# A spiking-recommender kernel: five gather tiles for three, the identity built first, small reciprocals, 15 table chunks held

## The chip, the core and the metric

The kernel runs on one core of a Trainium2 chip. The core has five engines that run side by side and meet at semaphores: TensorE (PE in the profile; its weight loads are PEld), VectorE (DVE), ScalarE (ACT), GpSimd (POOL) and SyncE (SP). SP and POOL issue DMAs, which run on the core's 16 DMA engines. The metric is device time in microseconds (us) of one execution, median of several runs.

## What is computed

The reference takes sequences of item numbers (1024 x 50), their lengths, and a table of 100,001 embeddings of 128 numbers. Cut to what matters:

```python
emb = emb_table.at[0].set(0.0)
prefix = jnp.cumsum(emb[seq], axis=1)                 # over the 50 steps
uF = prefix / jnp.minimum(t_idx, lengths)[:, :, None]
y = (uF - mean) * rsqrt(var + eps) * gamma + beta     # mean and var over the 1024 sequences
v = v + (x - v) / 2; spike = (v >= 1); v = v - spike  # one step of the scan over t, x = y[:, t]
uF_out = spikes.mean(axis=0)
scores = uF_out @ emb.T                               # 1024 x 100001
```

## The kernel before

**Two stages.** The first runs over the 50 steps and ends with `countR`, the number of spikes of every dimension (128 partitions) and sequence (1024 columns). The second multiplies `countR` with the whole table and writes the 409.6 MB of scores. The order of instructions on each engine is the program's own (`manual_schedule`); every engine takes its queue in order. Buffers come from pools that hand tiles out in rotation: a tile's writer waits until the last reader of that buffer's earlier tile is done.

**Setup.** SP loads the item numbers `idx` (L106), the lengths spread to all partitions, `len_i` of 128 x 1024 (L108), row 0 of the table, gamma and beta, and then issues `fetch` for the first `AHEAD` = 16 chunks of the table (2048 rows, 1 MB each). POOL issues `gather(0)` and then builds the identity `ident` that TensorE transposes with. VectorE builds `isz` (which places hold item 0), TensorE transposes it (L143), VectorE copies it to `zT` (L145). `rlen`, the reciprocal of the lengths, is worked out on 128 x 1024 by a conversion (L157) and a reciprocal (L158).

**One step t of the first stage.** POOL gathers step t+1 (L209 calls `gather`, L122): eight indirect DMAs, each of 128 table rows, into a tile `e` of 128 x 1024, from a pool of three tiles. `isz` is a tile of that pool too. TensorE transposes the tile's eight blocks into two PSUM banks `pre`, where the running sum over the steps stands (L219). VectorE scales each half to `uF` (L228) and takes its statistics (L229). TensorE subtracts row 0's part for the next step (`correct`, L179, two matmuls) and adds the spikes of the step before to `count` (L189, two matmuls). VectorE and ScalarE then do the normalisation and the neuron's update (L233 to L267) on 128 x 1024. So a step has twelve matmuls, each with its own weight load. In the steps t = 40, 42, 44 and 46 `prepare` (L90 to L92) follows: eight transposes of table rows on TensorE, a copy `hi` on ScalarE and a rest `lo` on VectorE. They stand in the queues ahead of the transposes of steps 41, 43, 45 and 47.

**The second stage** takes 49 chunks of 2048 table rows. For each of eight blocks of 128 sequences, TensorE multiplies (L301), VectorE and ScalarE take turns at moving results to `o` (L309, L311), and SP writes 1 MB to `scores` (L313). After the fifth block of a chunk SP issues `fetch` for the chunk that lies `AHEAD` further on, into the tile of a chunk that has been used.

Of the kernel before, what the change touches and what calls it, by code (L numbers as in the profile page):

```python
# [12 lines left out]
F32 = mybir.dt.float32  # L13
BF16 = mybir.dt.bfloat16
F32R = mybir.dt.float32r
I32 = mybir.dt.int32
# [4 lines left out]
P = 128  # L21
BN_EPS = 1e-5
V_TH = 1.0
CH = 2048
AHEAD = 16
HALF = 1024
BANK = 512

# [2 lines left out]
def rec_kernel(  # L31
# [9 lines left out]
    nc = tc.nc  # L41
    B, T = seq.shape
    N, D = table.shape
    NB = B // P
# [6 lines left out]
    embp = ctx.enter_context(tc.tile_pool(name="embT", bufs=4))  # L51
    rowp = ctx.enter_context(tc.tile_pool(name="rows", bufs=AHEAD))


    countR = const.tile([P, B], F32R, tag="countR", name="countR")
    ident = const.tile([P, P], F32, tag="ident", name="ident")
# [5 lines left out]
    def fetch(c0):  # L62
        w = min(CH, N - c0)
        full, rest = divmod(w, P)
        r = rowp.tile([P, CH // P, D], F32, tag="rows", name=f"rows_{c0}")
        if full:
            nc.sync.dma_start(
                out=r[:, :full, :],
                in_=table[c0 : c0 + full * P, :].rearrange("(k p) d -> p k d", p=P),
            )  # L70
        if rest:
            nc.sync.dma_start(out=r[:rest, full, :], in_=table[c0 + full * P : c0 + w, :])
        rows[c0] = r

    def prepare(c0, h0, pt):


        w = min(CH, N - c0)
        hw = min(HALF, w - h0)
        r = rows[c0]  # L80
        if c0 == 0 and h0 == 0:
            nc.vector.memset(r[0:1, 0, :], 0.0)
        hi = embp.tile([P, HALF], F32R, tag="hi", name=f"hi_{c0}_{h0}")
        lo = embp.tile([P, HALF], F32R, tag="lo", name=f"lo_{c0}_{h0}")
        if hw % 2:
            nc.vector.memset(hi[:, hw : hw + 1].bitcast(F32), 0.0)
            nc.vector.memset(lo[:, hw : hw + 1].bitcast(F32), 0.0)
        for k0 in range(0, hw, P):
            kw = min(P, hw - k0)
            nc.tensor.transpose(pt[:, k0 : k0 + kw], r[:kw, (h0 + k0) // P, :], ident[:kw, :kw])  # L90
        nc.scalar.copy(hi[:, :hw], pt[:, :hw])  # L91
        nc.vector.tensor_tensor(lo[:, :hw], pt[:, :hw], hi[:, :hw].bitcast(F32), ALU.subtract)  # L92
        split[c0, h0] = hi, lo


    with ExitStack() as ph:
        once = ph.enter_context(tc.tile_pool(name="once", bufs=1))
        gp = ph.enter_context(tc.tile_pool(name="gather", bufs=3))
        up = ph.enter_context(tc.tile_pool(name="uF", bufs=2))
        sp = ph.enter_context(tc.tile_pool(name="stats", bufs=3))  # L100
        lp = ph.enter_context(tc.tile_pool(name="lif", bufs=2))
# [1 line left out]
        vp = ph.enter_context(tc.tile_pool(name="v", bufs=1, space=bass.MemoryType.PSUM))  # L103

        idx = once.tile([P, NB, T], I32, tag="idx", name="idx")
        nc.sync.dma_start(out=idx, in_=seq.rearrange("(n p) t -> p n t", p=P))  # L106
        len_i = up.tile([P, B], I32, tag="uF", name="len_i")
        nc.sync.dma_start(out=len_i, in_=lengths.rearrange("(o b) -> o b", o=1).to_broadcast([P, B]))  # L108
        r0 = once.tile([P, D], F32, tag="r0", name="r0")
        nc.sync.dma_start(out=r0, in_=table[0:1, :].to_broadcast([P, D]))  # L110
        gb = once.tile([P, 2], F32, tag="gb", name="gb")
# [1 line left out]
        nc.sync.dma_start(out=gb[:, 1:2], in_=beta.rearrange("(d o) -> d o", o=1))  # L113
        for c0 in range(0, min(AHEAD * CH, N), CH):
            fetch(c0)
# [3 lines left out]
        def gather(t):  # L119
            es[t] = gp.tile([P, B], F32, tag="e", name=f"e_{t}")  # L120
            for n in range(NB):
                nc.gpsimd.indirect_dma_start(  # L122
                    out=es[t][:, n * P : (n + 1) * P],
                    out_offset=None,
                    in_=table,
                    in_offset=bass.IndirectOffsetOnAxis(ap=idx[:, n, t : t + 1].bitcast(U32), axis=0),
                )

        gather(0)
        make_identity(nc, ident)  # L130
        ident_h = once.tile([P, P], BF16, tag="ident_h", name="ident_h")
        nc.vector.tensor_copy(ident_h, ident)

# [7 lines left out]
        zps = vp.tile([P, B], F32, tag="v1", name="zps")  # L141
        for n in range(NB):
            nc.tensor.transpose(zps[:, n * P : (n + 1) * P], isz[:, n, :], ident)  # L143
        zT = once.tile([P, B], F32R, tag="zT", name="zT")
        nc.vector.tensor_copy(zT, zps)  # L145
        r0hi = once.tile([P, D], F32R, tag="r0hi", name="r0hi")
        nc.scalar.copy(r0hi, r0)
        r0n = once.tile([P, D], F32, tag="r0n", name="r0n")
# [4 lines left out]
        nc.vector.tensor_tensor(sel, ident[:, : P // 2], ident[:, P // 2 :], ALU.add)  # L153


        rlen = once.tile([P, B], F32, tag="rlen", name="rlen")
        nc.vector.tensor_copy(rlen, len_i)  # L157
        nc.vector.reciprocal(rlen, rlen)  # L158

        hgb = once.tile([P, 2], F32, tag="hgb", name="hgb")  # L160
        nc.vector.tensor_scalar_mul(hgb, gb, 0.5)
# [45 lines left out]
        for t in range(T):  # L207
# [3 lines left out]
            e = es.pop(t)  # L211
# [3 lines left out]
            uF = up.tile([P, B], F32, tag="uF", name=f"uF_{t}")  # L215
# [74 lines left out]
    for c0 in range(0, N, CH):  # L290
        w = min(CH, N - c0)
        for n in range(NB):
            o = op.tile([P, CH], F32, tag="o", name=f"o_{c0}_{n}")
# [21 lines left out]
            if n in (1, 4) and c0:  # L315
                h0 = 0 if n == 1 else HALF
                if nxt + h0 < N:
                    prepare(nxt, h0, psum.tile([P, HALF], F32, tag="ps", name=f"pt_{nxt}_{h0}"))
            if n == 4 and c0 + AHEAD * CH < N:
                fetch(c0 + AHEAD * CH)  # L320

# [18 lines left out]
```

## Time and profile before

| what | value |
|---|---|
| median of 3 runs (lowest, highest) | 1724.94 us (1724.48, 1726.58) |
| the profiled execution | 1723.19 us, span 1721.3 us |
| first stage: until the writing of scores sets in | 598.5 us, the first 68 us of it beside the loading of 16 chunks |
| second stage | 1122.8 us |
| busy: PE, DVE, ACT, POOL | 1141.8, 969.4, 636.3, 379.5 us |
| POOL's gathers | 400 x 947 ns |
| moved by DMA | 488.75 MB, of it 409.60 MB written to HBM |

The profile is of one execution. A group of instructions is named by its line, engine, operation and tiles (out<-in). After its busy time stand the engine's idle time before it and what ended that; "remote" means that no instruction in the profile fits the semaphore that ended the wait, "issue" that the engine waited for nothing that the profile shows. [...] The step t is also called tile t, after its tile of gathered rows.

### The profile page before, as it was taken

The numbers are of one execution on the slowest core, as the hardware profiler recorded it, in microseconds if no ns is written. First come the engines' busy times: TensorE is split into PE (matmuls) and PEld (weight loads), VectorE is DVE, ScalarE is ACT, GpSimd is POOL, SyncE is SP. The second block draws the span as 40 slices with busy tenths as digits, with TensorE's granted clock in tenths as the row PEclk, the third lists the DMA queues.
The fourth block names the chain that finished last, engine by engine and source line by source line (L and its number), as shares of the span: only waits on it lengthen the run. The fifth ranks groups of instructions, "written<-read, shape, count | busy, mean of one in ns | idle before, by whom it ended". The sixth has DMA issues, their size and how long they took to land.

```text
span 1721.3 us, 13874 instructions
## 1 busy us (share of the span) xinstructions
PE 1141.8 (66%) x4526; PEld 820.3 (48%) x4526; DVE 969.4 (56%) x1261; ACT 636.3 (37%) x698; POOL 379.5 (22%) x406
## 2 busy tenths in 40 slices
PE   2233333433344478877788777877778888888886
PEld 1112222221222356655566555666556666666664
DVE  5557756765667645554455444554445555555554
ACT  1222222221223344443444434444334444444443
POOL 7666666666666000000000000000000000000000
PEclk9855555555555599999999999998998899999999
DMA  9811111111111199999999999999999999999998
GB/s 267 234 44 48 48 48 44 48 49 46 45 49 46 38 391 397 401 400 393 388 394 402 394 391 393 395 400 390 396 396 390 403 410 414 402 405 406 403 402 349
DMA packets 98004, 488.75 MB, mean 284 GB/s; under 512 B 14827, under 2 KB 16652, under 8 KB 48780
## 3 DMA queue, kind: packets, MB, share of 16 engines
q1 hardware_dynamic: 85132, 461.63, 68.9%
q0 software_dynamic: 12800, 26.24, 5.3%
q8 instruction: 35, 0.57, 0.1%
q14 instruction: 37, 0.30, 0.0%
HBM read 78.21 MB, written 409.60 MB: 283 GB/s over the span
## 4 chain that ended last, share of the span: by engine, by line
DMA 48%; DVE 23%; PE 10%; another core or an unknown queue 9%; ACT 5%; issue 4%; POOL 0%; ACTq 0%; DVEq 0%; SPq 0%
DMA scores<-o 48%; PE po L301 9%; DVE bs L229 4%; ACT o L311 4%; DVE uF L228 4%; DVE v L267 3%; DVE s L199 3%; DVE negv L266 2%; DVE o L309 2%; ACT v L264 1%; DVE mv L233 1%; DVE a L257 1%; DVE r L255 1%; DVE q L254 0%
## 5 line engine op out<-in xcount | busy, mean ns | idle before, releaser
L301 PE MATMUL po<-hi,countR 128*128 128x512 f32 x1568 | 679.9, 434 | 179.5 <-ACT o L311 176.4
L309 DVE TENSOR_SCALAR o<-po 128x1024 f32<-128x1024 f32 x392 | 478.9, 1222 | 460.3 <-DMA scores<-o 428.3
L301 PE MATMUL po<-lo,countR 128*128 128x512 f32 x1568 | 645.0, 412 | 0.0
L311 ACT ACTIVATE o<-po 128x1024 f32<-128x1024 f32 (+1 forms) x392 | 399.9, 1020 | 633.2 <-DMA scores<-o 506.0
L301 PEld LDWEIGHTS po<-hi,countR 128*128 128x128 f32 x1568 | 316.0, 202 | 330.5 <-ACT o L311 243.0
L122 POOL DMA_INDIRECT e<-in_L_rec_emb_table,idx x400 | 378.8, 947 | 184.7 <-issue 109.3
L301 PEld LDWEIGHTS po<-lo,countR 128*128 128x128 f32 x1568 | 316.4, 202 | 60.1
L179 PE MATMUL pre<-zT,l 128*128 128x512 f32 x100 | 72.7, 729 | 264.4 <-DVE uF L228 196.0
L179 PEld LDWEIGHTS pre<-zT,l 128*128 128x128 f32 x100 | 27.0, 271 | 306.0 <-issue 192.2
L92 DVE TENSOR_TENSOR lo<-pt,hi 128x1024 fp32r<-128x1024 f32 x98 | 119.7, 1221 | 87.9 <-ACT hi L91 86.2
L228 DVE SCALAR_TENSOR_TENSOR uF<-rlen,pre 128x512 f32<-128x512 f32 x100 | 67.9, 679 | 144.8 <-remote 129.3
L237 ACT ACTIVATE r<-mv,eps 128x1 f32<-128x1 f32 x50 | 14.7, 295 | 351.4 <-DVE mv L233 307.2
L90 PE MATMUL pt<-ident,rows 128*128 128x128 f32 x782 | 108.4, 283 | 19.3 <-ACT o L311 12.0
L90 PEld LDWEIGHTS pt<-ident,rows 128*128 128x128 f32 x782 | 89.2, 144 | 52.4 <-ACT o L311 38.2
L189 PE MATMUL count<-s,ident_h 128*128 128x512 bf16 x100 | 50.7, 608 | 88.9 <-DVE s L199 67.8
L91 ACT CAST hi<-pt 128x1024 fp32r<-128x1024 f32 x98 | 98.5, 1005 | 16.1 <-remote 11.3
L219 PEld LDWEIGHTS pre<-ident,e 128*128 128x128 f32 x400 | 86.7, 228 | 21.3 <-issue 18.6
L219 PE MATMUL pre<-ident,e 128*128 128x128 f32 x400 | 95.4, 418 | 0.0
L264 ACT ACTIVATE v<-uF,hgb,a 128x1024 f32<-128x1024 f32 (+1 forms) x51 | 60.8, 1192 | 52.0 <-DVE r L255 16.2
L229 DVE BATCH_NORM_STATS2 bs<-uF 128x6 f32<-128x512 f32 x100 | 69.4, 694 | 3.4
L267 DVE SCALAR_TENSOR_TENSOR v<-negv,v 128x1024 f32<-128x1024 f32 (+1 forms) x51 | 61.6, 1209 | 15.6 <-issue 7.3
L189 PEld LDWEIGHTS <-ident_h 128*128 128x128 bf16 x100 | 12.2, 122 | 103.2 <-issue 102.9
(41 smaller groups left out, 286.3 us busy)
## 6 DMA issues: line engine op xcount, KB each, us to landing
scores<-o SPq DMA_DIRECT2D x384, 1024.0 KB
scores<-o SPq DMA_DIRECT2D x8, 848.5 KB
e<-in_L_rec_emb_table,idx POOLq DMA_INDIRECT x400
rows<-in_L_rec_emb_table SPq DMA_DIRECT2D x1, 832.0 KB
rows<-in_L_rec_emb_table SPq DMA_DIRECT2D x48, 0.5 KB
len_i<-in_r_lengths SPq DMA_DIRECT2D x1, 512.0 KB
idx<-in_r_seq SPq DMA_DIRECT2D x1, 200.0 KB
r<-in_L_rec_emb_table SPq DMA_DIRECT2D x1, 64.0 KB
```

The lines of the kernel that those rows point to most:

```text
L90: nc.tensor.transpose(pt[:, k0 : k0 + kw], r[:kw, (h0 + k0) // P, :], ident[:kw, :kw])
L91: nc.scalar.copy(hi[:, :hw], pt[:, :hw])
L92: nc.vector.tensor_tensor(lo[:, :hw], pt[:, :hw], hi[:, :hw].bitcast(F32), ALU.subtract)
L122: nc.gpsimd.indirect_dma_start(out=es[t][:, n * P : (n + 1) * P], out_offset=None, in_=table, in_offset=bass.IndirectOffsetOnAxis(ap=idx[: ...
L179: nc.tensor.matmul(pre[h], lhsT=l, rhs=zT[:, h * BANK : (h + 1) * BANK], start=t == 0, stop=False, skip_group_check=True,)
L219: nc.tensor.matmul(pre[h][:, k : k + P], lhsT=e[:, h * BANK + k : h * BANK + k + P], rhs=ident, start=False, stop=last, is_transpose=True, ...
L228: nc.vector.scalar_tensor_tensor(uF[:, cs], rlen[:, cs], 1.0 / (t + 1), pre[h], ALU.max, ALU.mult)
L229: nc.vector.bn_stats(bs[:, h, :], uF[:, cs])
L267: nc.vector.scalar_tensor_tensor(vt[:, cs], negv[:, cs], -0.5, vt[:, cs], ALU.mult, ALU.add)
L301: nc.tensor.matmul(po[:, k0 : k0 + kw], lhsT=countR[:, n * P : (n + 1) * P], rhs=part[:, k0 : k0 + kw], start=j == 0, stop=j == 1,)
L309: nc.vector.tensor_scalar_mul(o[:, h0 : h0 + hw], po[:, :hw], 1.0 / T)
L311: nc.scalar.mul(o[:, h0 : h0 + hw], po[:, :hw], 1.0 / T)
```

## The change

The pool of gathered tiles has five tiles, and `AHEAD` is 15, so 15 chunks of the table are held. `make_identity` stands ahead of `gather(0)` in POOL's queue. The lengths are loaded as 128 x 8 (one length for every partition and block), converted and inverted in that shape, spread by a copy to `rb` (128 x 1024, a tile of the gather pool), transposed by eight transposes on TensorE, and copied from PSUM to `rlen`. The copy to `zT` goes from VectorE to ScalarE. Nothing in the loop over t or in the second stage is edited.

```diff
-AHEAD = 16
+AHEAD = 15
...
-        gp = ph.enter_context(tc.tile_pool(name="gather", bufs=3))
+        gp = ph.enter_context(tc.tile_pool(name="gather", bufs=5))
...
-        len_i = up.tile([P, B], I32, tag="uF", name="len_i")
-        nc.sync.dma_start(out=len_i, in_=lengths.rearrange("(o b) -> o b", o=1).to_broadcast([P, B]))
+        len_i = once.tile([P, NB], I32, tag="len_i", name="len_i")
+        nc.sync.dma_start(out=len_i, in_=lengths.rearrange("(n p) -> p n", p=P))
...
+        make_identity(nc, ident)
         gather(0)
-        make_identity(nc, ident)
...
-        nc.vector.tensor_copy(zT, zps)
+        nc.scalar.copy(zT, zps)
...
+        rl = once.tile([P, NB], F32, tag="rl", name="rl")
+        nc.vector.tensor_copy(rl, len_i)
+        nc.vector.reciprocal(rl, rl)
+        rb = gp.tile([P, NB, P], F32, tag="e", name="rb")
+        nc.vector.tensor_copy(rb, rl.unsqueeze(2).to_broadcast([P, NB, P]))
+        rps = vp.tile([P, B], F32, tag="v0", name="rps")
+        for n in range(NB):
+            nc.tensor.transpose(rps[:, n * P : (n + 1) * P], rb[:, n, :], ident)
         rlen = once.tile([P, B], F32, tag="rlen", name="rlen")
-        nc.vector.tensor_copy(rlen, len_i)
-        nc.vector.reciprocal(rlen, rlen)
+        nc.vector.tensor_copy(rlen, rps)
```

## The prediction

> **What bounds the kernel now.** First I cut the span in three by windows: the chunk loads, the rest of the 50 steps, the writing of scores.
>
> ```profile
> core 0: us, PE busy (x) PEld busy (x) DVE busy (x) ACT busy (x) POOL busy (x), PEclk, DMA share, GB/s
> 0.00:68.00 68.00, 17.17 (x53) 11.32 (x53) 33.19 (x59) 12.16 (x17) 45.33 (x53) 1.00 1.00 275
> 68.00:598.50 530.50, 205.58 (x599) 126.13 (x600) 351.34 (x716) 140.57 (x196) 334.15 (x354) 0.53 0.17 48
> 598.50:1721.30 1122.80, 919.01 (x3876) 682.89 (x3874) 584.85 (x487) 483.57 (x485) 0.00 (x0) 0.94 1.00 396
> ```
>
> The last stretch is bound by DMA (share 1.00). In the middle one nothing is full: DMA 0.17, DVE 351 of 530 us, POOL 334. Something waits; POOL's waits say how much:
>
> ```profile
> engine line waited for: us in total, times, longest us
> POOL e L122 <- issue: 109.3, 358, 0.6
> POOL e L122 <- remote: 64.4, 16, 5.4
> ```
>
> Sixteen stalls of some 4 us: the first gather of a tile waits for its buffer, that is for TensorE's transposes of three tiles earlier. One stall in the timeline:
>
> ```profile
> 112.60 1.91 PE L219 MATMUL pre<-ident,e 128*128 128x128 f32 x8
> ...
> 122.25 0.95 POOL L122 DMA_INDIRECT e<-in_L_rec_emb_table,idx  x1 [0.30 <-issue]
> 122.79 0.69 DVE L228 SCALAR_TENSOR_TENSOR uF<-rlen,pre 128x512 f32<-128x512 f32 x1 [7.54 <-remote]
> ...
> 127.05 0.69 DVE L228 SCALAR_TENSOR_TENSOR uF<-rlen,pre 128x512 f32<-128x512 f32 x1 [2.84 <-remote]
> ...
> 127.29 0.95 POOL L122 DMA_INDIRECT e<-in_L_rec_emb_table,idx  x1 [4.09 <-remote]
> ```
>
> This is tile 8. Its rows were gathered from 93.49 to 103.2, and TensorE's records of its eight transposes stand at 112.60 to 114.5. Yet VectorE's two halves, which wait for TensorE alone, start at 122.79 and 127.05. The semaphore events of the trace explain it: TensorE's completions of these transposes arrive at 115.06, 117.86, 119.96, 122.77 and 125.56, some 2.5 us apart (two of POOL's 1.25 us gathers), and the rest within 0.1 us at 127.0, which is 3.8 us after POOL's last gather ended (123.2). So POOL does not merely wait for TensorE: while POOL gathers, TensorE's completions are held back, and they come free when POOL stops. It stops only because its three tiles are full. VectorE's starts in the timeline show the cycle:
>
> ```profile
> 127.05 0.69 DVE L228 SCALAR_TENSOR_TENSOR uF<-rlen,pre 128x512 f32<-128x512 f32 x1 [2.84 <-remote]
> ...
> 134.79 0.67 DVE L228 SCALAR_TENSOR_TENSOR uF<-rlen,pre 128x512 f32<-128x512 f32 x1
> ...
> 142.52 0.67 DVE L228 SCALAR_TENSOR_TENSOR uF<-rlen,pre 128x512 f32<-128x512 f32 x1
> ...
> 160.90 0.69 DVE L228 SCALAR_TENSOR_TENSOR uF<-rlen,pre 128x512 f32<-128x512 f32 x1 [2.85 <-remote]
> ```
>
> Two tiles in 7.74 and 7.73 us, the third in 18.38: 33.85 us for three tiles, of which POOL gathers 30 and stalls 4. From a release to the next holding TensorE always does about 27 matmuls (two tiles and the rest of one); the first holding comes in tile 2, after 32.
>
> [...] the gather issued at 122.25 has landed at 124.35. So late data is not what holds tile 8. [...] gathers follow each other every 1.25 us whether VectorE is busy (128 to 143) or idle (116 to 122). [...]
>
> **The change part by part.**
>
> *Identity first.* Its two POOL instructions (0.23 and 0.29 us, 0.75 with gaps, 13.65 to 14.40) leave the gap between gathers and go where POOL waits 3.36 us for `idx`. Gain 0.44 us at every later gather.
>
> *Lengths.* The spread load (512 KB, 1.8 us at the 290 GB/s of the loads) becomes 1024 runs of 4 bytes; the nearest row is `idx`, 1024 runs of 200 bytes, which landed 2.8 us after issue. Even 20 us would be hidden: rlen is first used with tile 0, whose last rows land at 18.6. VectorE loses a conversion (0.85) and a reciprocal (6.55) and the zT copy (1.23), and gains a conversion (0.1), a reciprocal of 8 columns (0.15 for one column, and 6.4 ns a column from the large one: 0.2), the copy to rb (0.85 to 1.23) and the copy to rlen (1.23). TensorE gains eight transposes (1.94), ScalarE the zT copy (1.0). Setup ends some 10 us sooner. I take nothing for it: tile 1's rows land at 28.6 and tile 2's at 39.4, and tile 2's transposes already started at 40.62. If that cover went, it would be worth 1 to 9 us.
>
> *15 chunks.* One chunk's load moves into the DMA-bound stage. Windows with and without loads:
>
> ```profile
> 598.00:1330.00 732.00, 588.64 (x2458) 445.90 (x2457) 369.00 (x306) 307.15 (x307) 0.00 (x0) 0.92 1.01 394
> 1345.00:1700.00 355.00, 311.80 (x1342) 222.81 (x1341) 201.24 (x169) 166.45 (x167) 0.00 (x0) 0.99 0.99 405
> ```
>
> A chunk is 8.39 MB of scores and 1.05 MB of table: 9.44 MB at 394 GB/s is 23.95 us, 8.39 at 405 is 20.7. Cost +3.2 us. That the loads of the first stage end 4 us earlier is hidden, they end at 68 anyway.
>
> *Five tiles.* A larger pool lets POOL run longer before it stops, and TensorE is released only when it stops. At the start: the new transposes bring the 32 matmuls eight earlier, so the first holding falls in tile 1, at about 28. The rotation (e0, isz, rb, e1, e2, then e3 in e0's buffer) makes POOL wait for tile 1 before gathering tile 6, for tile 2 before 7, for tile 3 before 8: at 64, 74 and 84 us. A held tile takes 12 x 2.45 = 29 us; tile 1 is done at about 45, tile 2 at about 75. So POOL stops first at tile 7 or 8, and the release comes at 78 with tile 2 or at 88 with tile 3, where before tile 2 came at 59.6 and tile 3 at 67.6. VectorE is then 18 to 20 us late, and POOL starts tile 8 at 88 instead of 93.49: 5 us ahead. From there the cycle is the old one: a release, two quick tiles, a holding, POOL fills its last free tile and stops 30 us after its restart. Still 33.85 us for three tiles, only with TensorE five tiles behind POOL, not three.
>
> At the end POOL's last gather, 563.5 to 564.5, comes 5 us earlier. The last release followed it by 1.9 us (566.34) and completed tile 47; tiles 48 and 49 were left. Now it completes tile 45, and 46 to 49 are left. The two more cost 2 x 7.73, and a prepare that TensorE does ahead of tile 47: in step 43 it put the transposes at 6.94 us after the second half of uF instead of 3.9, +3.0. Together 18.5 - 5 = +13.5 us.
>
> **Sum.** 1723.2 (the profiled execution) + 3.2 + 13.5 = 1739.9. The median of the runs is 1.7 above the profiled one, so 1741.6.
>
> **The rivals.** *POOL becomes the bound.* If holding depends on TensorE finding POOL's buffers full, five tiles end it: 400 gathers at 1.25 us from 3.8 end at 504, the 34 us from last gather to the scores give 538, 60 us sooner, with the chunk's 3.2: 1668. For it speaks that 64.4 us of stall are the whole of POOL's surplus time. Against it: releases follow POOL's stop, not the other way round. It decides if fewer than some 4 matmuls a tile are still open when the next tile comes, what POOL's 10 us a tile let through at 2.45. *Only the chunk.* VectorE catches up in the tail, or the first holding stays short: 1723 to 1729, about 1728. *Worse holding.* If TensorE is held anew in every tile, a tile takes 10 of gathering and 3.8 of release, 13.8 instead of 11.3: up to +125, 1850; a few such tiles give +20 to +40. *The change doesn't do what it says*, because isz and rb take two of the five tiles: only at the start, both are read before 15 us.
>
> **How the numbers follow.** A measurement tells 0.2% (3.4 us) from no change. Longer tail 0.63 (its own range 1732 to 1752: POOL 0 to 9 us ahead, two tiles 15.5 to 22); only the chunk 0.09, mostly within 0.2%; POOL bound 0.18; worse holding 0.10, half of it under 1768. From 1722 to 1768 lie 0.63 + 0.09 + 0.05 and the faint ends of both: about 0.8. Faster 0.18, same 0.08, slower 0.74.
>
> **What would show it.** POOL's stalls stay at about 4 us every third tile, 15 of them, the first at tile 7 or 8; VectorE's first long wait comes in tile 1 or 2 and lasts to 78 or 88; POOL's last gather at 558 to 560, scores from about 612; 34 chunks at 23.9 us instead of 33. I am wrong if POOL stalls for under 20 us in all, or if VectorE's cycle is not near 33.85.

## The result, and the profile after

The changed kernel takes 1745.94 us in the median of 4 runs (1745.77 to 1747.90); the kernel before, with one run more, takes 1725.36 us (1724.48 to 1726.58). The ratio is 1.0121, 95% interval 1.0104 to 1.0139: 20.6 us slower. The forecast was 1741.6 us.

The windows of the changed kernel, cut at 64 us, 4 us sooner than in before since one chunk less is loaded first, and at 612.5, 6 us ahead of the first scores: columns are length, busy time and count of each engine, granted clock, DMA share, GB/s.

```profile
core 0: us, PE busy (x) PEld busy (x) DVE busy (x) ACT busy (x) POOL busy (x), PEclk, DMA share, GB/s
0.00:64.00 64.00, 17.25 (x49) 9.72 (x49) 19.98 (x44) 10.22 (x14) 46.21 (x54) 0.63 1.00 269
64.00:612.50 548.50, 204.10 (x598) 124.44 (x599) 356.47 (x727) 141.90 (x197) 333.11 (x353) 0.54 0.18 46
612.50:1744.20 1131.70, 934.66 (x3887) 702.71 (x3886) 586.29 (x491) 485.15 (x488) 0.00 (x0) 0.91 1.00 394
```

The middle stage is longer and the engines do hardly more in it: DVE 356 us for 351, POOL 333 for 334. Scores set in at 618.4 instead of 598.5 (+19.9), and writing them takes 1125.8 us instead of 1122.8 (+3.0). The waits of POOL, columns us in total, times, longest:

```profile
POOL e L122 <- issue: 114.1, 374, 0.3
POOL e L122 <- remote: 65.2, 15, 9.7
```

Fifteen stalls stand for sixteen, with the same 65 us. The timeline shows the first stall and the beginning of the cycle:

```profile
87.27 0.69 DVE L235 SCALAR_TENSOR_TENSOR uF<-rlen,pre 128x512 f32<-128x512 f32 x1 [15.20 <-remote]
...
93.56 0.69 DVE L235 SCALAR_TENSOR_TENSOR uF<-rlen,pre 128x512 f32<-128x512 f32 x1 [4.87 <-remote]
...
93.80 0.95 POOL L122 DMA_INDIRECT e<-in_L_rec_emb_table,idx  x1 [9.66 <-remote]
...
101.30 0.67 DVE L235 SCALAR_TENSOR_TENSOR uF<-rlen,pre 128x512 f32<-128x512 f32 x1
...
116.88 0.69 DVE L235 SCALAR_TENSOR_TENSOR uF<-rlen,pre 128x512 f32<-128x512 f32 x1 [2.86 <-remote]
...
117.11 0.95 POOL L122 DMA_INDIRECT e<-in_L_rec_emb_table,idx  x1 [3.61 <-remote]
```

The uF halves at 87.27 and 93.56 are tile 3; POOL stands ready to gather tile 8 into its buffer from 84.1 on and gets it at 93.80, after 9.66 us. From 116.88 the cycle is the old one, 33.8 us for three tiles (releases at 150.70, 184.57, 218.40). The end of the stage, first in before, from the start of POOL's last gather on:

```profile
563.52 0.95 POOL L122 DMA_INDIRECT e<-in_L_rec_emb_table,idx  x1 [0.30 <-issue]
566.34 0.69 DVE L228 SCALAR_TENSOR_TENSOR uF<-rlen,pre 128x512 f32<-128x512 f32 x1 [2.79 <-remote]
...
574.09 0.67 DVE L228 SCALAR_TENSOR_TENSOR uF<-rlen,pre 128x512 f32<-128x512 f32 x1
...
584.33 0.67 DVE L228 SCALAR_TENSOR_TENSOR uF<-rlen,pre 128x512 f32<-128x512 f32 x1
```

These are the second halves of tiles 47, 48 and 49. The changed kernel:

```profile
564.18 0.94 POOL L122 DMA_INDIRECT e<-in_L_rec_emb_table,idx  x1 [0.31 <-issue]
...
567.78 0.69 DVE L235 SCALAR_TENSOR_TENSOR uF<-rlen,pre 128x512 f32<-128x512 f32 x1 [2.15 <-remote]
...
575.52 0.67 DVE L235 SCALAR_TENSOR_TENSOR uF<-rlen,pre 128x512 f32<-128x512 f32 x1
...
586.20 0.67 DVE L235 SCALAR_TENSOR_TENSOR uF<-rlen,pre 128x512 f32<-128x512 f32 x1
...
593.93 0.67 DVE L235 SCALAR_TENSOR_TENSOR uF<-rlen,pre 128x512 f32<-128x512 f32 x1
```

These are the second halves of tiles 45, 46, 47 and 48; tile 49 follows at 604.18. So POOL ends at the same time, and VectorE then has four tiles more to do where it had two. From the start of the last gather to the first scores it takes 54.2 us instead of 35.0.

### The profile page after: what moved, and what is told of

Read it like the earlier page. It is cut to its first block, busy times and chain, and to the rows that moved or that the text cites. A ratio compares the mean times of both kernels' runs of the same rounds, so it can differ in the third digit from the quotient of the medians.

```text
span 1744.2 us, 13891 instructions
## 1 busy us (share of the span) xinstructions
PE 1156.0 (66%) x4534; PEld 836.9 (48%) x4534; DVE 962.8 (55%) x1262; ACT 637.3 (37%) x699; POOL 379.3 (22%) x406
## 4 chain that ended last, share of the span: by engine, by line
DMA 45%; DVE 22%; PE 13%; another core or an unknown queue 10%; ACT 4%; issue 3%; POOL 1%; SPq 0%; ACTq 0%; DVEq 0%
DMA scores<-o 44%; PE po L308 13%; DVE bs L236 4%; DVE uF L235 3%; ACT o L318 3%; DVE v L274 3%; DVE s L206 3%; DVE negv L273 3%; DVE o L316 2%; POOL e L122 1%; PE pt L90 1%; DVE mv L240 1%; DVE a L264 1%; ACT v L271 1%
## 5 line engine op out<-in xcount | busy, mean ns | idle before, releaser
L308 PE MATMUL po<-hi,countR 128*128 128x512 f32 x1568 | 688.0, 439 | 173.4 <-ACT o L318 171.0
L308 PE MATMUL po<-lo,countR 128*128 128x512 f32 x1568 | 654.8, 418 | 0.0
L308 PEld LDWEIGHTS po<-hi,countR 128*128 128x128 f32 x1568 | 323.3, 206 | 317.2 <-ACT o L318 229.6
L308 PEld LDWEIGHTS po<-lo,countR 128*128 128x128 f32 x1568 | 323.3, 206 | 62.7
```

The costliest lines, as they stand in the source:

```text
L308: nc.tensor.matmul(po[:, k0 : k0 + kw], lhsT=countR[:, n * P : (n + 1) * P], rhs=part[:, k0 : k0 + kw], start=j == 0, stop=j == 1,)
```

## The experiments

Twelve experiments ran, with ten different kernels (one of them three times), on five chips, and the chips turned out to be of two kinds. On some, the kernel before takes 1725 to 1728 us, as in the result; on others 1645. The two kinds are called A and B here. Each of the five chips was used in one set of experiments only, so whether the kind belongs to the chip or to its state at the time is not known. Each experiment has the kernel before beside it on its own chip, and only such pairs are compared, except where two traces are set side by side by name.

### One part alone, on a chip of kind B

Five tiles and 15 chunks, the setup as before:

```diff
-AHEAD = 16
+AHEAD = 15
-        gp = ph.enter_context(tc.tile_pool(name="gather", bufs=3))
+        gp = ph.enter_context(tc.tile_pool(name="gather", bufs=5))
```

> The kernel before with five gather tiles and 15 chunks; the setup (identity, reciprocal, zT) stays as it was. Tail theory (more tiles, TensorE further behind when POOL stops for good): 18 to 21 us slower than before, as the whole change, with the scores setting in at about 617 and POOL's last gather at 562 to 566. Rival, the setup edits cost it: about 3 us slower, the chunk alone.

The setup edits alone, against the changed kernel:

```diff
-AHEAD = 15
+AHEAD = 16
-        gp = ph.enter_context(tc.tile_pool(name="gather", bufs=5))
+        gp = ph.enter_context(tc.tile_pool(name="gather", bufs=3))
-        rb = gp.tile([P, NB, P], F32, tag="e", name="rb")
+        rb = up.tile([P, NB, P], F32, tag="uF", name="rb")
```

> The setup edits alone (identity first, lengths on 128x8, zT on ScalarE): three gather tiles, 16 chunks, and rb in a buffer of uF instead of the gather pool. Tail theory: within 4 us of before, scores from 595 to 602, stalls of POOL 15 or 16 of about 4 us. Rival, the setup edits cost it: 17 us slower.

Four tiles, against the changed kernel:

```diff
-        gp = ph.enter_context(tc.tile_pool(name="gather", bufs=5))
+        gp = ph.enter_context(tc.tile_pool(name="gather", bufs=4))
```

> The changed kernel with four gather tiles. Tail theory: TensorE is four tiles behind instead of five when POOL stops, so one tile of 7.7 us less in the tail: 8 to 14 us slower than before. Rival, anything over three tiles does the whole harm at once (or none does): as the changed kernel, 20 us slower, or about 3.

Five tiles with the wait of three, against the changed kernel:

```diff
         def gather(t):
+            if t > 2:
+                nc.gpsimd.memset(es_all[t - 3][0:1, 0:1], 0.0)
```

> The changed kernel with its five gather tiles, but ahead of the gathers of tile t POOL clears one element of tile t-3, which TensorE must have read: POOL stops where three tiles would have stopped it. Tail theory: what costs is how far POOL gets ahead, so 2 to 8 us slower than before, scores from about 600. Rival, the larger pool itself costs (addresses, memory): as the changed kernel, about 20 us slower.

Measured, beside a kernel before of 1645.43 us:

| kernel | us | ratio, 95% interval |
|---|---|---|
| five tiles, 15 chunks | 1648.71 | 1.0020 (1.0013 to 1.0027) |
| setup edits alone, 16 chunks | 1644.78 | 0.9996 (0.9987 to 1.0005) |
| the change with four tiles | 1648.03 | 1.0016 (1.0009 to 1.0023) |
| the change with the wait of three | 1647.95 | 1.0015 (1.0008 to 1.0022) |

The tail theory expected 18 to 21 us of the first and 8 to 14 of the third; both missed, since nothing is held on this chip. The other two came out as expected, which for the same reason says as little. POOL's waits with five tiles there:

```profile
POOL e L122 <- issue: 116.3, 382, 0.3
POOL e L122 <- DMA idx<-in_r_seq: 3.4, 1, 3.4
```

No stall is left but the one for `idx`. The gathers run from 3.9 to 504 without a break, scores set in at 520.7, and POOL is the bound: the case that the prediction put at 0.18, but brought about by the chip, and with three tiles too. In none of the four kernels does POOL wait longer than 0.3 us at a time, `idx` aside, so neither a larger pool nor one more wait can matter there. The three kernels with 15 chunks are 2.5 to 3.3 us slower, the one with 16 is 0.7 faster, which is within the noise. In the traces the scores set in at 520.5 to 520.7 in all four; only the second stage differs, 1125.1 to 1125.7 us with 15 chunks and 1122.1 with 16. So that is the chunk, and the setup edits cost nothing here. On the 20 us this set says nothing.

### The changed kernel again, and counting on VectorE: kind A

The changed kernel, unedited:

> The changed kernel itself, beside the kernel before on the same chip. In the first four experiments the kernel before took 1645.4 us instead of 1725, and no completion of TensorE was held back. Theory (holding makes the 20 us, the chunk the rest): where the kernel before takes about 1725 this one is 20 us slower, with POOL's stalls every third tile; where it takes about 1645 nothing is held and this one is 2 to 4 us slower, the chunk alone. Rival (the 20 us do not come from the holding): 15 to 20 us slower in both.

The kernel before with 15 chunks, spikes summed on VectorE:

```diff
-        count = [accp.tile([P, BANK], F32, tag=f"count{h}", name=f"count{h}") for h in range(B // BANK)]
+        count = once.tile([P, B], BF16, tag="count", name="count")
...
-            nc.tensor.matmul(
-                count[h],
-                lhsT=ident_h,
-                rhs=s[:, h * BANK : (h + 1) * BANK],
...
+            nc.vector.tensor_tensor(count[:, cs], count[:, cs], s[:, cs], ALU.add)
```

> The kernel before with 15 chunks, and the spikes counted on VectorE in a bf16 tile of SBUF instead of two TensorE matmuls a step, so ten matmuls a tile instead of twelve. Theory: where the kernel before takes about 1725, the holding comes after 2.7 tiles instead of 2.25, and it is 4 to 9 us faster than before in spite of the chunk's 3 us; where it takes about 1645, VectorE is not the bound of the first stage, so 2 to 5 us slower (the chunk, and the last count). Rival (the number of matmuls does not matter for the holding): 3 us slower or more in both.

The changed kernel: 1746.22 us against 1724.70, ratio 1.0118 (1.0101 to 1.0135). The result repeats on another chip of its kind. Counting on VectorE: 1727.10 us, 1.0011 (1.0003 to 1.0020), 2.4 us slower where 4 to 9 us faster was expected; the chunk's 3 us taken off, nothing was won. Its POOL:

```profile
POOL e L122 <- issue: 114.2, 374, 0.6
POOL e L122 <- remote: 40.8, 9, 5.3
POOL e L122 <- PE pre L178: 22.3, 8, 5.2
```

With ten matmuls a tile the stalls do come later, every fourth tile instead of every third. But each is longer, 5.1 us instead of 4.1, and their sum hardly moves: 62.1 us in fourteen stalls (the other 1.0 us of the two rows are three ordinary gaps), beside 64.4 and 65.2. This does not fit the picture of a fixed number of matmuls until a holding. Setting the stalls of the traces of kind A against the gathers since the stall before gave another one:

| gathers in a row | stall after them | where |
|---|---|---|
| 16 | 2.8 to 3.1 us | the last steps of before, of the changed kernel and of counting on VectorE (the changed kernel's second stall, also after 16, takes 3.6) |
| 24 | 4.1 us | before and changed kernel, steady cycle |
| 32 | 5.1 us | counting on VectorE, steady cycle |
| 64 | 9.7 us | the changed kernel's first stall |

From 24 to 64 gathers the stall grows by 5.6 us, 0.14 us a gather. A gather every 1.25 us and its share of the stalls come to 33.8 / 24 = 1.41 us, and 45.2 / 32 = 1.41 with counting on VectorE. The early stalls that the table leaves out fit it only as sums: before stalls 5.41 us after its first 40 gathers, the changed kernel again 6.70 after 56 and 5.18 after eight more, counting on VectorE 1.80 after 40 and 5.14 after eight more. From the first gather to the end of these stalls it is 1.40, 1.43 and 1.40 us a gather.

By these sums it looks as if something let gathers pass at no more than one in 1.41 us on these chips, with a backlog growing while POOL issues faster, and TensorE's completions waiting until the backlog is gone. Then POOL's pauses are no waste. By this estimate, whatever the buffers, tile 48 can start at about 4 + 384 x 1.41 = 545 and, as no stall follows, the last gather 15 x 1.25 us later, at 564; the traces of before and of the changed kernel have 544.8 and 545.4, 563.5 and 564.2. Only what is left to do after that can differ.

Such a backlog would not be one of transfers. Counted in order, the last DMA packet of a gather ends 2.13 us after POOL starts it in before, 2.20 in the changed kernel and 2.19 with five tiles on kind B (medians of gathers 60 to 380), and a long run of gathers makes it no later: 2.14 us for the 64th of the changed kernel, the last one ahead of its stall of 9.66 us. In before and in the changed kernel it is TensorE alone that is late: between 100 and 460 us its recorded semaphore events come up to 8.3 us after the last end of a matmul that signals, those of VectorE and ScalarE within 0.02 us. With counting on VectorE some of VectorE's are late too, by up to 2.1 us.

### Pacing, two tiles, no gathers: kind B again

Five tiles and 15 chunks, by the first diff above:

> The kernel before with five gather tiles and 15 chunks, setup as it was. Where the kernel before takes about 1725: tail theory 18 to 21 us slower, scores from about 617 and POOL's last gather still at 562 to 566; rival (the setup edits make the difference) about 3. Where it takes about 1645: about 3 slower, as in the first run of it.

The kernel before with its gathers paced:

```diff
+        idle = once.tile([P, 224], F32, tag="idle", name="idle")
...
                     in_offset=bass.IndirectOffsetOnAxis(ap=idx[:, n, t : t + 1].bitcast(U32), axis=0),
                 )
+                nc.gpsimd.memset(idle, 0.0)
```

> The kernel before with a memset of 128x224 on POOL behind every gather, so that a gather starts every 1.42 us or so instead of every 1.25. Theory (something serves the gathers at no more than one in 1.41 us, and TensorE's completions wait while a backlog stands): where the kernel before takes about 1725 no backlog forms, POOL's stalls of 64 us shrink below 15, VectorE follows POOL tile by tile, last gather at 570 to 580, scores 17 us later at 588 to 598, so 0 to 10 us faster. Rival, the theory of the prediction (completions are held while POOL is at work, and freed when it stops): the cycle of three tiles grows by 24 x 0.17 = 4 us, sixteen times: 50 to 65 us slower. Where the kernel before takes about 1645 POOL is the bound: 400 x 0.17 = 60 to 75 us slower under both.

The kernel before with two tiles:

```diff
-        gp = ph.enter_context(tc.tile_pool(name="gather", bufs=3))
+        gp = ph.enter_context(tc.tile_pool(name="gather", bufs=2))
...
-        isz = gp.tile([P, NB, P], F32, tag="e", name="isz")
+        isz = up.tile([P, NB, P], F32, tag="uF", name="isz")
```

> The kernel before with two gather tiles, isz in a buffer of uF, 16 chunks. Tail theory: TensorE is one tile less behind when POOL stops; POOL's last gather at 563 to 568, the tail 26 us instead of 34, 3 to 8 us faster where the kernel before takes about 1725. Rival (POOL stops too often, at its short stops it loses what the tail gains): 0 to 10 us slower. Where it takes about 1645, POOL never waits for a tile of two: within 2 us of before.

The kernel before with plain loads by SP in place of the gathers:

```diff
-                nc.gpsimd.indirect_dma_start(
+                nc.sync.dma_start(
                     out=es[t][:, n * P : (n + 1) * P],
-                    out_offset=None,
-                    in_=table,
-                    in_offset=bass.IndirectOffsetOnAxis(ap=idx[:, n, t : t + 1].bitcast(U32), axis=0),
+                    in_=table[(8 * t + n) * P : (8 * t + n + 1) * P, :],
                 )
```

> The kernel before, but the gather is left out: each of the 400 blocks of 128 rows is loaded by SP from consecutive rows of the table, so the scores are others; the number of transfers, their bytes, and everything TensorE, VectorE and ScalarE do stay. They queue behind the 16 chunk loads, so the first tile comes at about 64. Theory A (it is POOL's making of gathers that holds TensorE): nothing is held, VectorE's 7.73 us a tile bound the stage, scores at 450 to 475. Theory B (it is the completion events of the transfers, 128 a tile, which stay): TensorE is held as before or worse, scores later than 560. Where the kernel before takes about 1645, 450 to 475 under both.

Beside a kernel before of 1644.51 us: five tiles 1647.60, ratio 1.0019 (1.0011 to 1.0027); paced 1711.85, 1.0411 (1.0394 to 1.0429); two tiles 1644.74, 0.9999 (0.9991 to 1.0008); without gathers 1602.13 in a single run. This chip again held nothing, so the three with gathers only show POOL as the bound: the paced gathers start every 1.416 us, the last at 570.4 instead of 503, and scores follow 17.3 us later. Without gathers, scores set in at 478.2, a few us beyond the range expected; tiles then come every 7.73 us from the end of the chunk loads on. Whether SP's loads would hold TensorE on a chip of kind A, and whether two tiles help there, stays untried.

### Pacing the changed kernel: kind A

Against the changed kernel:

```diff
+        idle = once.tile([P, 240], F32, tag="idle", name="idle")
...
                     in_offset=bass.IndirectOffsetOnAxis(ap=idx[:, n, t : t + 1].bitcast(U32), axis=0),
                 )
+                nc.gpsimd.memset(idle, 0.0)
```

> The changed kernel with a memset of 128x240 on POOL behind every gather: a gather every 1.43 us. Theory (a backlog of gathers holds TensorE where the kernel before takes about 1725, and the five tiles cost only through it): no stall of POOL, scores at 592 to 598, 34 chunks with loads, so 1717 to 1726: within 0.5% of before and some 25 us less than the changed kernel. Rival (completions are held while POOL is at work and freed when it stops): POOL is at work longer, so 35 us or more slower than before. Where the kernel before takes about 1645, POOL is the bound and the chunk is added: 1718 to 1726 under both, 6 us over the paced kernel before with its 1.416 us.

1720.33 us against 1724.76, ratio 0.9973 (0.9962 to 0.9984): faster than the kernel before on that chip, and some 25 us below the changed kernel. POOL's waits and a piece of the timeline:

```profile
POOL e L123 <- issue: 66.7, 398, 1.0
POOL e L123 <- DMA idx<-in_r_seq: 2.5, 1, 2.5
```

```profile
120.12 0.95 POOL L123 DMA_INDIRECT e<-in_L_rec_emb_table,idx  x1 [0.17 <-issue]
120.26 0.69 DVE L237 SCALAR_TENSOR_TENSOR uF<-rlen,pre 128x512 f32<-128x512 f32 x1 [3.59 <-PE pre L228]
...
121.07 0.31 POOL L129 MEMSET idle<- 128x240 f32 x1
121.55 0.95 POOL L123 DMA_INDIRECT e<-in_L_rec_emb_table,idx  x1 [0.16 <-issue]
...
129.73 0.47 PE L228 MATMUL pre<-ident,e 128*128 128x128 f32 x1 [0.65 <-DMA e<-in_L_rec_emb_table,idx]
```

POOL never stalls for a buffer between 3.9 and 576, and TensorE is never held: VectorE's uF follows each tile's last transpose, every 11.4 us, TensorE waits for data, and between 100 and 460 us its recorded events come within 0.02 us of a matmul's end. By the rival, the prediction's own mechanism, this kernel had to be 35 us slower or more. So POOL's being at work is not what holds TensorE; how fast its gathers follow each other decides: 1.43 us a gather is slow enough, 1.25 is not. The memset also widens the gap between two gathers from 0.30 to 0.48 us, and this run does not tell the wider gap from the slower pace; the sums of 1.41 us a gather speak for the pace. The last gather starts at 575.6, 11.4 us later than in the changed kernel, and scores follow 17.0 us later, at 592.6. With pacing the tail of the five tiles is gone: the paced kernel before, with three tiles on kind B where nothing is held anyway, had 17.3 us in the same place.

### One part alone, on kind A at last

The kernel before with five tiles and 15 chunks once more:

```diff
-AHEAD = 16
+AHEAD = 15
-        gp = ph.enter_context(tc.tile_pool(name="gather", bufs=3))
+        gp = ph.enter_context(tc.tile_pool(name="gather", bufs=5))
```

> The kernel before with five gather tiles and 15 chunks, setup as it was; meant for a chip on which the kernel before takes about 1725. There, by the tail theory: 18 to 21 us slower, scores from about 617, POOL's last gather at 562 to 566, the last release of TensorE completing tile 44 or 45. Rival, the setup edits put TensorE behind: about 3 us slower, scores from about 599. On a chip where the kernel before takes about 1645: about 3 us slower under both, which tells nothing new.

1749.62 us against 1728.38, ratio 1.0123 (1.0106 to 1.0140): 21.2 us slower, the whole harm, without one setup edit.

```profile
559.18 0.69 DVE L228 SCALAR_TENSOR_TENSOR uF<-rlen,pre 128x512 f32<-128x512 f32 x1 [4.22 <-remote]
559.42 0.94 POOL L122 DMA_INDIRECT e<-in_L_rec_emb_table,idx  x1 [3.04 <-remote]
...
568.15 0.95 POOL L122 DMA_INDIRECT e<-in_L_rec_emb_table,idx  x1 [0.30 <-issue]
...
569.83 0.67 DVE L228 SCALAR_TENSOR_TENSOR uF<-rlen,pre 128x512 f32<-128x512 f32 x1
```

The release at 559.18 completes tile 44 and lets POOL gather the last tile; at 568.15, when its last gather starts, VectorE has yet to do tiles 45 (second half at 569.83) to 49, and scores set in at 620.2. POOL's last gather is 4.6 us later than in the kernel before of the result and 2 us beyond the range expected; this chip's stalls are a little longer all through (4.3 to 4.5 us every third tile). Its first stall is also at tile 8, after 64 gathers, and takes 8.47 us.

Side by side, from the start of POOL's last gather to the first scores:

| kernel | kind | last gather | scores from | between |
|---|---|---|---|---|
| before (the result's trace) | A | 563.5 | 598.5 | 35.0 |
| counting on VectorE, three tiles | A | 565.2 | 599.7 | 34.5 |
| changed kernel | A | 564.2 | 618.4 | 54.2 |
| changed kernel again | A | 565.0 | 619.1 | 54.1 |
| five tiles, setup as before | A | 568.1 | 620.2 | 52.1 |
| changed kernel, paced | A | 575.6 | 592.6 | 17.0 |
| five tiles, setup as before | B | 503.6 | 520.7 | 17.1 |

Three tiles against five make the last column wherever completions are held: 35 us against 52 to 54. The 15 chunks do not (counting on VectorE has them too), and the setup edits for no more than the 2 us between five tiles with them and without.

## Why the prediction was right, and where it was not

**Longer tail.** Right in kind, and in the size of its main term. Two more tiles and one more `prepare` behind the last release were put at 18.5 us; the traces have 53.2 us instead of 34.0 from the end of the last gather to the scores, so 19.2. The extra `prepare` was put at 3.0 us, and between tiles 46 and 47 the changed kernel takes 10.68 us (575.52 to 586.20) instead of 7.73. That it comes from the number of tiles is shown by five tiles without the setup edits, 21.2 us slower, the chunk included.

**POOL 5 us ahead.** This is the term that was mis-sized: POOL's last gather comes 0.7 us later, not 5 earlier, and these 5.7 us are most of the 6.4 by which the stage was under-estimated (+13.5 for +19.9). The step that failed is the release at 88, taken as 3.8 us after POOL's stop at 84, as if a stall had one length. The release came at 93.6, since a stall grows with the gathers before it: 64 gathers in a row, 9.66 us. The trace of before had this already: its sixteen stalls are not all of some 4 us, the first takes 5.41 after 40 gathers and the last two 2.89 and 2.99 after 16. From its first gather to the end of its first stall it takes 1.40 us a gather, and 64 x 1.40 us from the changed kernel's first gather at 4.2 gives 93.8, where tile 8 does start. Where POOL stops was right (tile 8, and tile 7 when the kernel ran again), though the steps that led there were not: tiles 1 and 2 were done at 32.7 and 65.6, not 45 and 75.

**The mechanism.** "Held while POOL gathers, free when POOL stops" describes before and is not the cause as it stands; the paced kernel gathers without a stop and is never held. What was found in its place is a rate, worked out as one gather in some 1.41 us; no run on kind A lies between 1.25 and 1.43. The tail came out right all the same, since with a rate, too, POOL ends when it did and leaves as many tiles as its pool has. The constant "27 matmuls" fell too: with ten matmuls a tile the stops moved, and POOL's sum of stalls stayed. The last gather comes within 2 us of 564 in four of the five unpaced kernels traced on kind A and at 568.1 in the fifth, as POOL's mean rate would have it whatever the pool or the number of matmuls.

**The chunk.** 3.2 us predicted, 3.0 in the changed kernel's second stage: 34 chunks of 23.9 us instead of 33, the others 20.9.

**Setup at nothing.** Right in the sum: lengths were ready at 13.4 instead of 27.6 and tile 0's first half started at 15.3 instead of 28.7, but tile 2 was done at 65.6 instead of 59.6, held. On kind B, where no holding takes the gain back, the setup edits are still worth no more than 0.7 us, within the noise, because POOL is the bound.

**The rivals.** "POOL becomes the bound" is what happens on every chip of kind B, with three tiles as with five, so the change gains nothing from it. The point given for it, fewer than four matmuls open when the next tile comes, was not tested by any run; the same five tiles met this rival on some chips and the longer tail on others. "Worse holding" did not come: the cycle is 33.8 us.

**What stays open.** What lets gathers pass at 1.41 us, and why only on some chips, is not settled, nor whether it counts gathers or something else that comes once a tile, since every tile has eight gathers. Two and four tiles, the wait of three, the setup edits alone and SP's loads ran on kind B only. One hint stands in the list of DMA issues; first the changed kernel, then the setup edits alone on kind B:

```profile
e<-in_L_rec_emb_table,idx POOLq DMA_INDIRECT x400
```

```profile
e<-in_L_rec_emb_table,idx POOLq DMA_INDIRECT x400, 2.5
```

The second ends with a median landing of 2.5 us, the first has none, because semaphore events that would tell it are not in the trace. On kind B the traces hold all 128 arrivals of a tile's gathers (8 gathers, 16 each); on kind A, between 64 and 500 us, about 25 in before and in the changed kernel, 23 with counting on VectorE, 84 in the paced one. So on kind A most events of this stage go unrecorded; but the paced kernel loses a third of them and holds nothing, so loss alone is not the holding. Lost semaphore events and late TensorE completions stand side by side on kind A (25 of 128 arrivals of a tile, up to 8.3 us), but no run here shows a link between them. Nor does any tell what the kernels take unrecorded: every run of this case, the timed ones too, comes with its span and clock. Where nothing is held, the change would cost some 3 us, the chunk alone: an estimate from kind B, where it is 2.5 to 3.3 us with four or five tiles.

## What to carry to other kernels

When an engine's stalls keep their sum while the buffers change (here 64.4 us with three tiles, 65.2 with five), ask for a rate behind them: plot each stall against the work since the stall before. One trace can be enough for a first look: the stalls of before differ in length, from 2.9 to 5.4 us, and their lengths follow the gathers ahead of them, 16 to 40. The deeper pool bought no throughput here (33.8 us for three tiles with both pools), and at the end of the stage the consumer had to work off what the pool had let the producer run ahead (54.2 us from the last gather to the scores instead of 35.0). Pacing the producer to just below that rate (1.43 us a gather, beside the estimate of 1.41) was worth more than the deeper pool: 0.3 us of idle work behind each gather turned a loss of 20 us into a gain of 4 on the chips that hold (the two measured on different ones), and cost the kernel before 67 us on those that do not, so measure on more than one chip before keeping it.

## What the runs showed of the hardware

- One kernel, two kinds of chips: 1725 to 1728 us on some, 1644.5 to 1645.4 on others, a difference of 80 us that lies in the gather stage (scores from 598.5 in before on A, from 520.7 with the setup edits alone on B). The second stage, with 16 chunks held, takes 1122.8 and 1122.1 us.
- On kind A TensorE's completions reach VectorE late, by up to 8.3 us in before and in the changed kernel, when POOL issues indirect gathers of 128 rows of 512 bytes every 1.25 us, while the gathers' own transfers stay on time (2.1 to 2.2 us from POOL's start). They come free 2.9 us after POOL's stop when 16 gathers went before it, 4.1 after 24, 5.1 after 32 and 9.7 after 64: about 0.7 us plus 0.14 us a gather, an estimate from these four. At one gather in 1.43 us they came within 0.02 us.
- On kind A only 7 of some 10.7 completion events of TensorE that kind B's traces have per tile are recorded, so the spacing of 2.5 us that the prediction read between them is an upper bound.
- A memset of 128x224 on POOL takes 0.30 us and one of 128x240 0.31; behind a gather they move the next one from 1.25 to 1.416 and 1.43 us, since some 0.13 of the 0.30 us between gathers absorbs part of them. A memset of one element (0.09 us) fits into that gap, and the next gather still starts 1.25 us after the one before.
